# One column of SiLU at the end of places that held exponentials or roots

## Chip, cores and metric

The kernel runs on one core of one Trainium2 chip. The metric is the device time of one execution in microseconds; 2289.83 us is the median of three runs of the kernel before the change (2289.25 to 2292.66).

## What is computed

Two layers on x of shape (4, 128, 64, 64), all in float32. Layer 0 is a convolutional attention with softmax over 4096 positions. Layer 1 works on the tokens: a causal attention with SiLU on keys and values, then a mixture of experts.

```
x = x + conv_attention(group_norm(x))
t = tokens(x)                                   # (4, 4096, 128)
kv = silu(layer_norm(t) @ W_kv.T)               # 8 heads of 128, keys and values
s = sum(q * k); m = cummax(s); e = exp(s - m)
t = t + mean_over_heads(cumsum(e * v) / cumsum(e))
t = t + experts(layer_norm(t))                  # softmax gate, top 8 tokens of each of 64 experts
```

## The kernel before

The tokens of layer 1 are worked off in 32 blocks of 512 (four batches of eight). `loop` (L2254) goes over n from 6 to 37: in step n the keys of block n are made, and the values, sums and outputs of block m = n - 6. The order of TensorE, ScalarE (ACT), VectorE (DVE) and GpSimd (POOL) is the order in which the program writes the calls; SyncE's (SP's) queue of DMAs is ordered by a scheduler.

A block has named places: slots 1 to 4 and V, W, D, O, T, G between them. Two things put work into places. `later` and `point` make a list of tasks due some slots later: `scan0` to `scan4` carry a running maximum and sum over a group of four blocks, and `scan2` (L1046) holds their exponential. `make_plan` fixes the gate's work beforehand: `gate_root` (L1245, a square root, mostly in slot 4 of every fourth block), `exps` (L1400 and L1402, exponentials of the gate), `gate_norm`, `gate_turn` (transposes L1289, copy L1290), `gate_logits` and others. `last_root` (L2165) is one more root, called behind slot 4 of block 6. `run(m, place)` calls what the plan has there.

`keys` (L975, L982) multiplies a 128-token chunk by the keys' weights into the PSUM tile f_pk, and an activation with SiLU on ACT empties it into f_e1a; VectorE multiplies by the query and sums (L983, L984). `value` (L1130, L1135) does the same for values: f_pv, SiLU, f_amb. f_pk and f_pv share two PSUM buffers, taken in turn. In a step the keys of chunks 0 and 1 come first, then slot 1 (with the gate's transposes, once they are running), the values of chunks 0 and 1, and so on.

SiLU, the exponential and the square root belong to different tables of ACT. Where two instructions that follow one another need different tables, the compiler puts an ACT_TABLE_LOAD between them; the profile gives it the line of the instruction for which it loads. Copies and the activation with Identity need no load.

Of the kernel before, what the change touches and what calls it, by code (L numbers as in the profile page):

```python
# [8 lines left out]
F32 = mybir.dt.float32  # L9
AF = mybir.ActivationFunctionType  # L10
# [3 lines left out]
P = 128  # L14
# [3 lines left out]
def conv_attn_hybrid_kernel(  # L18
# [24 lines left out]
    nc = tc.nc  # L43
# [20 lines left out]
    eps5 = const.tile([P, 1], F32, tag="eps5", name="eps5")  # L64
# [763 lines left out]
    def fast():  # L828
# [14 lines left out]
        NB = len(blocks)  # L843
        env = Env()
        env.tasks, env.now = [], 0

        def later(delay, fn):
            env.tasks.append((env.now + delay, fn))

        def point():  # L850
            env.now += 1
            due = [f for at, f in env.tasks if at <= env.now]
            env.tasks = [(at, f) for at, f in env.tasks if at > env.now]
            for f in due:
                f()
# [87 lines left out]
        def scan_at(i):  # L943
            return env.e1a[:, 2 * HD + i * P : 2 * HD + (i + 1) * P]
# [8 lines left out]
        def normals(n):  # L953
            b, k = blocks[n]
            xl_of[n] = xl = env.xl_pool(f"f_xl_{n}")
            for c in range(CPB):
                i = k * CPB + c
                nc.scalar.activation(  # L958
                    xl[:, c, :], t[:, b * NCH + i, :], AF.Identity,
                    bias=ln_nb[:, b, i : i + 1], scale=ln_rs[:, b, i : i + 1],  # L960
                )
# [8 lines left out]
        def keys(n, c):  # L970
            g = n // GB
            s = scan_at(g % 2).rearrange("p (i h) -> p i h", h=NH)
            pk = ps.tile([P, 2, BLK], F32, tag="kv", name=f"f_pk_{n}_{c}", bufs=2)
            for i in range(2):
                nc.tensor.matmul(  # L975
                    pk[:, i, :], xt_at(n)[:, bass.ts(c, P)], env.wks[:, bass.ts(i, BLK)],
                    start=True, stop=True,
                )
            flat = env.e1a[:, bass.ts(env.ks_count % 2, HD)]
            env.ks_count += 1  # L980
            ks = flat.rearrange("p (h c) -> p h c", h=NH)
            nc.scalar.activation(flat, pk.rearrange("p i x -> p (i x)"), AF.Silu)  # L982
            nc.vector.tensor_mul(ks, ks, env.qb)  # L983
            nc.vector.tensor_reduce(s[:, (n % GB) * CPB + c, :], ks, AX.X, ALU.add)  # L984
            if n % GB == GB - 1 and c == CPB - 1:
                later(2, lambda: scan0(g))
# [31 lines left out]
        def row_to_column(g, by_row, what):  # L1018
            pc = sm(f"f_{what}_{g}")
            nc.tensor.matmul(pc[:, 0:1], by_row, ones[0:1, 0:1], start=True, stop=True)  # L1020
            col = fc.tile([P, 1], F32, tag=what, name=f"f_{what}c_{g}", bufs=2)
            nc.vector.tensor_copy(col, pc[:, 0:1])
            return col
# [16 lines left out]
        def scan2(g):  # L1040
            top = row_to_column(g, group[g]["m"], "mc")
            nc.vector.scalar_tensor_tensor(
                out=scan_at(DD), in0=scan_at(MM), scalar=top, in1=scan_at(SS),
                op0=ALU.max, op1=ALU.subtract,
            )
            nc.scalar.activation(scan_at(ES), scan_at(DD), AF.Exp, scale=-1.0)  # L1046
            later(1, scan2b)
            later(3, lambda: scan3(g))

# [6 lines left out]
        def scan3(g):  # L1056
            group[g]["u"] = link_rows(g, ends_to_row(g, scan_at(UL), UR, "ur"), 1, UD)
            later(1, lambda: scan4(g))
# [62 lines left out]
        def weigh_rows(m):  # L1121
            em = ready[m][0].rearrange("p z x i -> p z (x i)")
            rb = env.e2a[:, HD:].rearrange("p (z x) -> p z x", z=HH)
            nc.vector.tensor_mul(em, em, rb)
# [115 lines left out]
        def ring(m):  # L1240
            return m % NBLK

        def gate_root(m, count):
            at = slice(ring(m), ring(m) + count)
            nc.scalar.activation(  # L1245
                env.grs[:, at], env.gmv[:, at, :, 1:2].rearrange("p m c o -> p m (c o)"),
                AF.Sqrt, bias=eps5,
            )
# [62 lines left out]
        def small_tile(b, what, *shape, dtype=F32, bufs=2):  # L1311
            return env.rest.tile([P, *shape], dtype, tag=what, name=f"f_{what}_{b}", bufs=bufs)

        def flat_lg(b, k0, k1):
            return env.lg[b][:, k0:k1, :].rearrange("p k x -> p (k x)")
# [77 lines left out]
                )  # L1393

        def exps(b, j):
            st = sel[b]
            if j == 0:
                st["ce"] = ce = small_tile(b, "ce", 6)[:, 0:5]
                st["sums"] = small_tile(b, "sums", 5, bufs=1)[:, 0:4]
                nc.scalar.activation(ce, st["src"][:, 0:5], AF.Exp, bias=st["neg"])  # L1400
            lg = flat_lg(b, CPB * j, CPB * j + CPB)
            nc.scalar.activation(  # L1402
                lg, lg, AF.Exp, bias=st["neg"], accum_out=st["sums"][:, j : j + 1]
            )
# [303 lines left out]
        def slot_of(room, i):  # L1708
            return room[:, bass.ts(i, HD)]
# [452 lines left out]
                point()  # L2162

        def last_root():
            nc.scalar.activation(  # L2165
                ln_rs[:, B - 1], ln_mv[:, B - 1, :, 1:2].rearrange("p i o -> p (i o)"), AF.Sqrt,
                bias=eps5,
            )
# [14 lines left out]
        def run(i, slot):  # L2183
            for fn, args in plan.pop((i, slot), []):
                fn(*args)
# [68 lines left out]

        def loop():
            make_plan()
            normals(LAG + 1)
            for n in range(LAG, NB + LAG):
                m = n - LAG

                def slot(p):
                    if n > LAG or p > 1:
                        point()
                    run(m, p)

                if n > LAG and n < NB:
                    keys(n, 0)
                    keys(n, 1)
                slot(1)
                if m:  # L2270
                    weigh_rows(m)
                value(m, 0)
                run(m, "V")
                value(m, 1)
                slot(2)
                run(m, "W")
                if n < NB:
                    keys(n, 2)
                    keys(n, 3)
                else:  # L2280
                    value(m, 2)
                open_block(m)
                totals(0)
                if n < NB:
                    totals(1)
                    products(m, 0)
                run(m, "D")
                if 2 <= m < 6:
                    for i in range(CPB):
                        tile_stats(env.rest, B - 1, (m - 2) * NBLK + i)  # L2290
                slot(3)
                if n < NB:
                    value(m, 2)
                value(m, 3)
                if n + 1 < NB:
                    tokens(n + 1)
                if n + 2 < NB:
                    normals(n + 2)
                slot(4)
                if m == 6:  # L2300
                    last_root()
                if n >= NB:
                    totals(1)
                    products(m, 0)
                totals(2)
                run(m, "O")
                totals(3)
                close_totals(m)
                run(m, "T")
                if m + 1 < NB:  # L2310
                    weights(m + 1)
                for x4 in range(1, CPB):
                    products(m, x4)
                outputs(m)
                gate_stats(m)
                if 2 <= m < 6:
                    for i in range(CPB, 2 * CPB):
                        tile_stats(env.rest, B - 1, (m - 2) * NBLK + i)
                run(m, "G")
                if n == NB - 1:  # L2320
                    for room in (env.wks, env.held[:, bass.ts(2, HD)], slot_of(env.e1a, 0),
                                 slot_of(env.e1a, 1)):
                        load_into(room)
                if n == NB + 2:
                    load_into(slot_of(env.e1a, 2))
                    load_into(slot_of(env.ama, 2))
                if n == NB + LAG - 2:
                    for room in (slot_of(env.e1a, 3), slot_of(env.ama, 0), slot_of(env.e2a, 0)):
                        load_into(room)
            while env.tasks:  # L2330
                point()
            assert not plan, plan.keys()
# [101 lines left out]
```

## Time and profile before

| what | value |
|---|---|
| median of three runs | 2289.83 us |
| profiled execution, its own time | 2288.86 us |
| its span in the profile | 2287.0 us |
| granted TensorE clock, mean | 0.995 |
| ACT_TABLE_LOAD, one | 1283 ns |
| SiLU of keys or values, 128x1024, one | 1025 ns |
| value matmuls L1130, busy and idle before | 239.4 and 6.2 us |

The span is the stretch that the profile's instructions fill; 1.9 us of the execution lie around it. A row of the profile gives line, engine, operation and tiles, then the number of instructions, busy time and the mean of one in ns, and after the second bar the idle time of the engine before them and what ended it. Layer 0 fills the span up to about 1515 us, the attention loop goes on to about 2180 us, the experts to about 2257 us, and the stores of the output end it.

### The profile page before, as it was taken

The page shows a single profiled execution, that of the slowest core. Times are in us where ns is not written, and L with a number is a line of the kernel's source. Part 1 is how long each engine was busy: PE and PEld are TensorE (multiplying, and loading weights), DVE is VectorE, ACT ScalarE, POOL GpSimd, SP SyncE. Part 2 cuts the span into 40 slices and gives each one's busy share as a digit, 9 for nine tenths or more (in the row PEclk, how much of TensorE's full clock was granted, in tenths as well). Part 3 has the DMA queues.
Part 4 walks back from the last instruction along what each step waited for, and adds up shares of the span by engine and source line. Part 5 has one row for each costly group of instructions (what it writes and reads, how often), then busy time and mean ns, then how long its engine had stood idle before and what let it go on. Part 6 is the DMA issues. An engine that isn't in the chain of part 4 may idle for free. (4 is left out here: it accounts for less than half of the span.)

```text
span 2287.0 us, 42915 instructions
## 1 busy us (share of the span) xinstructions
PE 2223.4 (97%) x18224; PEld 1147.4 (50%) x18224; DVE 1460.2 (64%) x2380; ACT 1091.6 (48%) x1328; POOL 175.9 (8%) x380
## 2 busy tenths in 40 slices
PE   7999999999999999999999999999999999999997
PEld 3644444444444444444444444456556555666663
DVE  7666665655666556556555666667877777776643
ACT  3344334443433443334444554445565676565651
POOL 0000000000000000000000000012121121223311
PEclk9999999999999999999999999999999999999999
DMA  2100010000010000001000000020211211313589
GB/s 68 42 12 12 14 46 9 17 9 9 9 53 9 9 9 17 9 9 44 9 5 5 5 5 10 6 49 27 65 45 40 67 50 41 95 55 110 169 298 343
DMA packets 79418, 108.95 MB, mean 48 GB/s; under 512 B 9072, under 2 KB 44912, under 8 KB 78960
## 3 DMA queue, kind: packets, MB, share of 16 engines
q1 hardware_dynamic: 78128, 104.01, 14.6%
q8 instruction: 145, 2.38, 0.4%
q0 software_dynamic: 512, 1.05, 0.2%
q10 hardware_dynamic: 576, 1.05, 0.1%
q14 instruction: 57, 0.47, 0.1%
HBM read 80.64 MB, written 19.14 MB: 44 GB/s over the span
## 5 line engine op out<-in xcount | busy, mean ns | idle before, releaser
L2033 PE MATMUL av<-pr,am 64*128 64x512 f32 x4096 | 980.0, 593 | 8.1 <-ACT pr L2013 8.1
L2013 ACT ACTIVATE pr<-sc 128x1024 f32<-128x1024 f32 x512 | 523.9, 1025 | 779.4 <-PE sc L2008 763.4
L2020 DVE TENSOR_TENSOR acc<-acc,pr 128x1024 f32<-128x1024 f32 x480 | 587.4, 1224 | 472.3 <-ACT pr L2013 468.7
L2033 PEld LDWEIGHTS av<-pr,am 64*128 64x128 f32 x4096 | 402.1, 187 | 480.3 <-issue 455.7
L2008 PE MATMUL sc<-e,e 64*128 64x512 f32 x2048 | 536.7, 593 | 3.9 <-DMA e<-side 3.9
L2008 PEld LDWEIGHTS sc<-e,e 64*128 64x128 f32 x2048 | 202.7, 188 | 236.5 <-issue 230.9
L1130 PE MATMUL f_pv<-f_held,f_ama 128*32 128x256 f32 x4096 | 239.4, 383 | 6.2 <-ACT f_e1a L982 5.1
L975 PE MATMUL f_pk<-f_held,f_ama 128*128 128x512 f32 x512 | 234.5, 602 | 0.0
L1135 ACT ACTIVATE f_amb<-f_pv 128x1024 f32<-128x1024 f32 x128 | 131.1, 1025 | 133.3 <-PE f_pv L1130 131.3
L983 DVE TENSOR_TENSOR f_e1a<-f_e1a,f_held 128x1024 f32<-128x1024 f32 x128 | 156.5, 1223 | 44.1 <-ACT f_e1a L982 43.8
L982 ACT ACTIVATE f_e1a<-f_pk 128x1024 f32<-128x1024 f32 x128 | 129.8, 1025 | 108.5 <-PE f_pk L975 54.4
L1130 PEld LDWEIGHTS f_pv<-f_held,f_ama 128*32 128x32 f32 x4096 | 129.9, 110 | 101.8 <-issue 12.0
L984 DVE TENSOR_REDUCE f_e1a<-f_e1a 128x8 f32<-128x1024 f32 x128 | 155.3, 1218 | 3.5
L975 PEld LDWEIGHTS f_pk<-f_held,f_ama 128*128 128x128 f32 x512 | 92.5, 190 | 108.3 <-issue 100.9
L1094 POOL COPY f_held<-f_e1a 32x32 f32<-32x32 f32 x128 | 30.7, 240 | 900.3 <-DVE f_e1a L1076 553.5
L1153 PE MATMUL f_pt<-f_amb,f_held 128*32 128x128 f32 x1920 | 84.1, 277 | 0.8 <-ACT f_amb L1135 0.8
L920 POOL MEMSET f_held<- 128x1024 f32 x1 | 1.0, 957 | 1033.6 <-DVE xn L1946 1033.6
L1153 PEld LDWEIGHTS f_pt<-f_amb,f_held 128*32 128x32 f32 x1920 | 60.4, 109 | 10.5 <-issue 5.2
L1194 DVE TENSOR_TENSOR t<-t,f_po 128x512 f32<-128x512 f32 (+1 forms) x33 | 22.1, 671 | 56.4 <-PE f_po L1188 56.4
L958 ACT ACTIVATE f_xl<-t,ln_nb,ln_rs 128x128 f32<-128x128 f32 x128 | 52.9, 491 | 0.8 <-PE pa L1981 0.8
L1277 ACT ACTIVATE f_x<-t,f_gnb,f_grs 128x128 f32<-128x128 f32 x122 | 49.7, 483 | 0.4 <-DVE f_grs L1255 0.4
L2017 DVE COPY acc<-pr 128x1024 f32<-128x1024 f32 x32 | 22.2, 694 | 39.3 <-ACT pr L2013 39.3
(304 smaller groups left out, 1777.4 us busy)
## 6 DMA issues: line engine op xcount, KB each, us to landing
f_e2a<-f_rd SPq DMA_DIRECT2D x128, 128.0 KB, 3.1
xr<-in_xtok_dram SPq DMA_DIRECT2D x32, 256.0 KB, 2.8
f_table<-f_x SPq DMA_DIRECT2D x62, 128.0 KB, 2.5
out_dram<-t SPq DMA_DIRECT2D x14, 512.0 KB, 3.8
x<-in_x_dram SPq DMA_DIRECT2D x12, 512.0 KB, 4.8
e<-e SPq DMA_DIRECT2D x32, 128.0 KB, 2.2
f_ama<-f_rd SPq DMA_DIRECT2D x16, 256.0 KB, 3.9
f_e1b<-f_rd SPq DMA_DIRECT2D x16, 256.0 KB, 4.1
```

The source lines that it names most:

```text
L958: nc.scalar.activation(xl[:, c, :], t[:, b * NCH + i, :], AF.Identity, bias=ln_nb[:, b, i : i + 1], scale=ln_rs[:, b, i : i + 1],)
L975: nc.tensor.matmul(pk[:, i, :], xt_at(n)[:, bass.ts(c, P)], env.wks[:, bass.ts(i, BLK)], start=True, stop=True,)
L982: nc.scalar.activation(flat, pk.rearrange("p i x -> p (i x)"), AF.Silu)
L983: nc.vector.tensor_mul(ks, ks, env.qb)
L984: nc.vector.tensor_reduce(s[:, (n % GB) * CPB + c, :], ks, AX.X, ALU.add)
L1130: nc.tensor.matmul(pv[a * CH : (a + 1) * CH, i, :], xt_at(m)[:, bass.ts(c * NA + i, CH)], env.wvs[:, bass.ts(a, HH * C)], start=True, stop ...
L1135: nc.scalar.activation(env.amb[:, bass.ts(c, HD)], pv.rearrange("p i x -> p (i x)"), AF.Silu)
L1153: nc.tensor.matmul(env.pt[i * CH : (i + 1) * CH, :], lhs, rhs, start=i not in env.begun, stop=False, skip_group_check=True,)
L2008: nc.tensor.matmul(sc[:, u, :], e2[halves[u], p, :], e1[halves[u], cols], start=True, stop=True,)
L2013: nc.scalar.activation(pr, sc, AF.Exp)
L2020: nc.vector.tensor_add(acc, acc, pr)
L2033: nc.tensor.matmul(av, am[h, j, :], pr[h, u, :], start=(j == 0), stop=(j == NCH - 1))
```

## The change

A one-column scratch tile and a flag are added. Every function that uses an exponential or a root on ACT sets the flag. At the end of slots 1 to 4 and of the places D and G, if the flag is set, ACT gets an activation with SiLU on one column (`eps5`, written to the scratch tile) and the flag is cleared; the last block is left out. `last_root` is called inside slot 4, before the new instruction.

```
+        def silu_table():
+            if env.other:
+                nc.scalar.activation(env.spare, eps5, AF.Silu)
+            env.other = False
+
         def gate_root(m, count):
+            env.other = True
...
         def loop():
             make_plan()
+            env.spare = env.rest.tile([P, 1], F32, tag="spare", name="f_spare")
+            env.other = False
...
                     run(m, p)
+                    if p == 4 and m == 6:
+                        last_root()
+                    if m + 1 < NB:
+                        silu_table()
...
                 run(m, "D")
+                if m + 1 < NB:
+                    silu_table()
...
                 slot(4)
-                if m == 6:
-                    last_root()
...
                 run(m, "G")
+                if m + 1 < NB:
+                    silu_table()
```

`env.other = True` is also added to `scan2` (behind its exponential), `exps` and `last_root`. 18 instructions are added in all.

More of the change, by code (lines that the diff above doesn't have):

```diff
@@ L1241, in ring @@
             return m % NBLK
+        def silu_table():
+            if env.other:
+                nc.scalar.activation(env.spare, eps5, AF.Silu)
+            env.other = False
         def gate_root(m, count):
+            env.other = True
             at = slice(ring(m), ring(m) + count)
@@ L1395, in exps @@
         def exps(b, j):
+            env.other = True
             st = sel[b]
@@ L2164, in last_root @@
         def last_root():
+            env.other = True
             nc.scalar.activation(
```

## The prediction

> **What bounds the kernel now.** I began with the page's engine table and the granted clock.
>
> ```profile
> PE 2223.4 (97%) x18224; PEld 1147.4 (50%) x18224; DVE 1460.2 (64%) x2380; ACT 1091.6 (48%) x1328; POOL 175.9 (8%) x380
> ```
>
> TensorE sets the time: 97% busy, its clock row at 9 in every slice. ScalarE (ACT) is about half idle, so what ACT does counts only where TensorE waits for it. The list of TensorE's waits says where that is:
>
> ```profile
> PE f_pv L1130 <- ACT f_e1a L982: 5.1, 14, 0.7
> ...
> PE f_pv L1130 <- ACT f_amb L1135: 0.9, 2, 0.8
> ...
> PE f_pt L1153 <- ACT f_amb L1135: 0.8, 2, 0.5
> ```
>
> Columns: microseconds in total, times, the longest. Value matmuls (L1130) wait 14 times for the keys' SiLU (L982), because keys and values share two PSUM buffers: the first value tile needs the buffer that the first key SiLU empties. To see what these 14 have in common I listed ACT's groups by line:
>
> ```profile
> L982 ACT ACT_TABLE_LOAD x21 | 26.9, 1283 | 17.3 <-issue 11.5 <-PE f_pk L975 5.7
> ...
> L1135 ACT ACT_TABLE_LOAD x5 | 6.4, 1283 | 3.3 <-PE f_pv L1130 3.2
> ...
> L1251 ACT ACTIVATE f_gnb<-eps 128x1 f32<-128x1 f32 x1 | 0.2, 203 | 0.0
> ```
>
> A table load takes 1283 ns. The last numbers of its row matter more: ACT is idle 17.3 us before the 21 loads of L982. The loads themselves wait for TensorE. One block of the loop, ACT in order of time, then TensorE over the same stretch:
>
> ```profile
> 1747.39 1.28 ACT L1046 ACT_TABLE_LOAD   x1
> 1748.68 0.31 ACT L1046 ACTIVATE f_e1a<-f_e1a 128x128 f32<-128x128 f32 x1
> 1750.34 1.28 ACT L982 ACT_TABLE_LOAD   x1 [1.35 <-PE f_pk L975]
> 1751.63 1.94 ACT L982 ACTIVATE f_e1a<-f_pk 128x1024 f32<-128x1024 f32 x2
> ```
>
> ```profile
> 1748.27 3.70 PE L975 MATMUL f_pk<-f_held,f_ama 128*128 128x512 f32 x8
> 1751.81 0.60 PE L1289 MATMUL f_gtr<-ident,f_x 128*128 128x128 f32 x4
> 1752.71 0.64 PE L1130 MATMUL f_pv<-f_held,f_ama 128*32 128x256 f32 x8 [0.30 <-ACT f_e1a L982]
> ```
>
> The exponential ends at 1748.99, ACT idles 1.35 us until the keys' product is there, and only then loads SiLU's table: SiLU starts 1.30 us late, its first tile is out at 1752.65, and TensorE goes on at 1752.71. A block without a load, for comparison:
>
> ```profile
> 1683.70 3.70 PE L975 MATMUL f_pk<-f_held,f_ama 128*128 128x512 f32 x8
> 1687.24 0.60 PE L1289 MATMUL f_gtr<-ident,f_x 128*128 128x128 f32 x4
> 1687.77 3.66 PE L1130 MATMUL f_pv<-f_held,f_ama 128*32 128x256 f32 x64
> ```
>
> From the first keys matmul to the first value matmul it takes 4.07 us here and 4.44 there: a block with a load loses 0.37 us (the 0.30 us gap plus the 0.07 us by which matmuls otherwise overlap).
>
> **The change, part by part.** The lists of instructions of both built programs show 18 added activations of one column on ACT and not one more table load (105 in each). Each of the 18 loads now stands before the small instruction, with no wait on it, where before it carried the wait for the product. TensorE, VectorE and POOL keep their order. Moving the root of the last batch into the place leaves ACT's order as it was.
>
> *The small instruction* has a row of the same form, L1251: 203 ns. Bounds: 0.1 us (neighbouring activations overlap by some 0.1 us in the timeline) to 0.3 us (the 128x5 exponential, 299 ns). After the end of the exponential or root ACT needs 0.02 + 1.28 + 0.20 minus some overlap, about 1.45 us, until it is ready for the next SiLU. Where it idled 1.2 us or more before the load this costs nothing; the cover is that idle time, and without it each place costs 0.1 to 0.3 us.
>
> *Fourteen places before key SiLUs*, from the timeline around each load (first keys to first value matmul):
> - Two early blocks (values at 1579.90, 1622.53), where no gate transposes stand between: 4.44 and 4.43 us against 3.63 without a load. ACT idled 1.38 and 1.24 us, so SiLU can start 1.1 to 1.2 us sooner, more than the 0.80 needed: 2 x 0.80 = 1.6 us.
> - Ten blocks like the one shown, 4.42 to 4.44 against 4.07, idle 1.03 to 2.76 us: 10 x 0.36 = 3.6 us.
> - One (1926.48) with an exponential of 1024 columns in the same place: idle only 0.23 us, so 0.23 - 0.15 = 0.08 us.
> - One (1663.39) with three loads in a row and no idle time: the small instruction comes on top, -0.14 us (-0.3 to 0).
>
> *Four late places* before value SiLUs: at 2096.43 the load goes into the 1.08 us in which ACT waited for a transpose, and the value wait of 0.756 us goes (+0.82 with the overlap); at 2119.34 nobody waits, 0; at 2149.11 ACT had 0.17 us to spare and the load now stands before a copy, -0.15; at 2157.08 ACT idled 0.85 us and a wait of 0.451 us at L1153 goes, +0.5.
>
> Sum: 1.6 + 3.6 + 0.08 - 0.14 + 0.82 - 0.15 + 0.5 = 6.3 us.
>
> *SP's queue* has one group of reorderings: in five blocks a store of the gate's table changes place with the third of four loads of f_e2a. The last of the four stays last, and in those blocks the VectorE product that reads them (L1124) starts 13.7 to 18 us after the last issue: 0.
>
> *The end.* Is the gain kept? I take all of it; the bounds are 0 and 6.3. The windows near the end:
>
> ```profile
> 2100.00:2190.00 90.00, 83.28 (x1574) 57.42 (x1566) 52.93 (x171) 58.28 (x88) 26.04 (x42) 0.96 0.56 177
> 2190.00:2200.00 10.00, 8.49 (x58) 4.60 (x58) 3.79 (x13) 5.91 (x12) 0.00 (x0) 0.83 0.42 126
> 2200.00:2250.00 50.00, 46.34 (x682) 30.08 (x682) 13.75 (x42) 21.28 (x48) 4.32 (x25) 1.00 1.04 372
> ```
>
> The last two columns are the DMA engines' share and GB/s. From 2200 the experts' weights fill the DMA engines (1.04), but this stretch starts with the first reload, issued at 2196.20 when the first expert matmuls (2194.26) free their room; before it the share is 0.56 and 0.42. So it starts earlier when TensorE comes earlier. The largest stall on the way, 2.56 us at 2133.08 for VectorE, hangs on a VectorE run that began at 2125.84 on TensorE's L1188, and shifts too.
>
> The profiled execution took 2288.86 us (span 2287.0 and 1.9 around it); less 6.3 that is 2282.6. The median is 0.97 above it, so 2289.83 - 6.3 = 2283.5.
>
> The Trainium skill (ScalarE: Activation LUTs, What ACT_TABLE_LOAD costs) gives a switch 1283 ns for the load and some 1380 ns of drain, 2.66 us together; here the load agrees and the drain isn't seen: the next activation starts 0.01 us after the load's end (1663.39 to 1664.68). By its figure each of the ten blocks would lose 1.38 us more than the 0.37 they do lose, and the estimate would be 14 us more gain, which the 4.44 us excludes.
>
> **Rivals.**
>
> *The end takes it back* (chance 0.15). TensorE waits 2.3 us for weights of the experts between 2238 and 2250; if preloads issued at 2175 to 2192 don't come earlier, the gain turns into such waits. All of it: 2289.8; half: 2286.7. Against it: those preloads wait in SP's queue for TensorE and ACT.
>
> *Nothing is gained* (0.05). The number of loads stays, ACT's busy time grows by 18 x 0.2 = 3.7 us; if the value matmuls were held by something else that comes at the same time, 2289.8. Against it: SiLU's first tile ends 0.06 us before every one of the waits. The Trainium skill (ScalarE: Activation LUTs, Table sets: the hidden batching unit) advises batching functions by set, which this change doesn't do; by that rule alone nothing is won.
>
> *Slower: the load doesn't go ahead* (0.10). If the small instruction is held as the SiLU was, behind ACT's own earlier instructions or a wait, the load stays where it is and 0.2 us comes on top at 17 places where TensorE waits or nearly does: 3.4 us, 2293.2, and with 0.3 us 2294.9. It decides where ACT's end of exponential plus 1.45 us passes the product's arrival by over 1 us. For it: the one place with three loads. Against it: loads without a wait start 0.02 us after the instruction before (1747.39).
>
> **How the numbers follow.** Forecast 0.70, the rivals 0.15, 0.05 and 0.10. The forecast's own range is 2282.0 to 2285.5. A measurement of this kernel can tell about 0.2% (4.6 us): faster is under 2285.25. Faster: 0.64 of the forecast and 0.02 of the first rival, 0.66. Slower: 0.07 of the last rival. The rest, 0.27, is the same. The range goes from 2281.5 (some 2 us more, if weight loads that wait on the same SiLU hide more) to 2290.5, which leaves the slower rival out.
>
> **What would show it.** Right: the wait of L1130 for L982 falls from 5.1 us to under 0.5 us, first keys to first value matmul is 4.07 us in the load blocks, the loads stand next to the exponential's end without idle time before them, and the first reload is issued some 6 us sooner. Wrong: the loads still start with the product's arrival, or the first reload comes sooner but waits for DMA grow at the experts (L1754, L1784).

## The result, and the profile after

| | before | after |
|---|---|---|
| median of 7 runs each | 2289.25 us (2285.61 to 2292.66) | 2280.07 us (2277.33 to 2283.81) |
| profiled execution, span | 2288.86, 2287.0 us | 2283.81, 2281.9 us |
| granted clock of that execution | 0.995 | 0.994 |

The ratio is 0.9962 with an interval of 0.9949 to 0.9974: 6.0 to 11.7 us less. A second series, in the experiments below, gave 0.9972 (0.9962 to 0.9983), 3.9 to 8.7 us. Both hold together between 6.0 and 8.7. The forecast said 6.3 us and 2283.5 us, with 2281.5 as the low end of its range; the first median lies 1.4 us below that end, the second (2281.68) just inside it. So the direction was right, and the size has to be explained.

The list of TensorE's waits of the changed kernel (microseconds in total, times, the longest):

```profile
PE f_pw L1334 <- DVE f_both L1347: 2.5, 1, 2.5
...
PE f_pl L1303 <- ACT f_spare L1246: 1.1, 1, 1.1
...
PE f_pv L1131 <- ACT f_e1a L982: 0.8, 2, 0.7
```

The 14 waits of 5.1 us for the keys' SiLU have become two of 0.8 us (the place with three loads has 0.7 of it). The 2.5 us for f_both have stayed. The 1.1 us in the middle are put down to the new instruction because its semaphore is the last one that the profile has; but what these matmuls follow in each of the two profiles is VectorE's L1307, by 0.14 to 0.15 us (its end at 2113.56 and their start at 2113.71 here), and in the second profile they start at 2112.67, ahead of the new instruction at 2113.31. The VectorE product before L1307 waited 5.7 us here for a DMA of f_e2a; in the second profile it waits 4.8 us, as in before, and TensorE 0.2: a late transfer of one execution.

ACT's groups of the changed kernel by line (count, busy us, mean ns of one; then the idle time before them):

```profile
L1246 ACT ACT_TABLE_LOAD x18 | 23.1, 1283 | 0.1
...
L982 ACT ACT_TABLE_LOAD x7 | 9.0, 1283 | 0.1
...
L1246 ACT ACTIVATE f_spare<-eps 128x1 f32<-128x1 f32 x18 | 3.7, 203 | 0.2
```

Of the 21 loads that stood at L982 after 17.3 us of idle time, 14 now stand at the new instruction, with 0.1 us of idle time before all 18 there. The new instruction takes 203 ns. The profile has 70 table loads in either kernel, so none was added; the 105 of the prediction was counted in the built programs, and no view of the profile shows that number.

The same block as in the prediction, ACT and then TensorE, in the changed kernel (start, duration, engine, line; in brackets the idle time before and what ended it):

```profile
1746.78 1.28 ACT L1046 ACT_TABLE_LOAD   x1
1748.08 0.31 ACT L1046 ACTIVATE f_e1a<-f_e1a 128x128 f32<-128x128 f32 x1
1748.39 1.28 ACT L1246 ACT_TABLE_LOAD   x1
1749.69 0.20 ACT L1246 ACTIVATE f_spare<-eps 128x1 f32<-128x1 f32 x1
1749.80 1.00 ACT L982 ACTIVATE f_e1a<-f_pk 128x1024 f32<-128x1024 f32 x1
```

```profile
1747.69 3.70 PE L975 MATMUL f_pk<-f_held,f_ama 128*128 128x512 f32 x8
1751.22 0.60 PE L1296 MATMUL f_gtr<-ident,f_x 128*128 128x128 f32 x4
1751.75 1.50 PE L1131 MATMUL f_pv<-f_held,f_ama 128*32 128x256 f32 x24
```

The load starts 0.01 us after the exponential's end, not 1.35 us later with the product. The first SiLU ends 3.11 us after the first keys matmul (1750.80 and 1747.69) and not 4.38 as before, so TensorE goes from the transposes straight to the values: from the first keys matmul to the first value matmul it is 4.06 us, where it was 4.44. In the two early blocks it is 3.63. One of the ten common blocks (values at 1972.74 in before) comes down only to 4.19 us, because two more matmuls of the gate (L1471) stand there between the transposes and the values.

**One ruler for all profiles.** The work up to the loop's second step takes 1533 to 1541 us in different executions, so spans hide a gain of some microseconds. The table below counts from the first value matmul of that step (1538.11 in the profile of before) to the same instruction of TensorE's order in each profile, found by aligning the orders. The mark at 2062.00 is the first value matmul of the last block that has keys; the text calls it the last keys. In microseconds:

```
mark (before's time)    before  before, again  after  after, again
1840.30                 302.19  302.18         299.21 299.21
2062.00, last keys      523.90  523.38         517.12 517.12
2100.57                 562.47  561.66         554.61 554.28
2160.02                 621.91  621.77         613.66 611.82
end of the program      748.89  748.11         742.55 740.71
```

Up to 1840 two profiles of one kernel agree to 0.01 us. The two columns of before differ at 2062 by 0.5 us through one gap of TensorE that only the first of them has. By this ruler the change gains 6.3 us until the last keys (523.4 less 517.1) and about 6.9 us until the end (748.5 less 741.6, each a mean of two; 6.3 to 8.2 by the pair taken).

**Why the clock has to be looked at.** The trace's record of the granted clock shows stretches at half rate, 3.41, 6.83 or 10.24 us long. In before two lie between 2100 and 2200 us, at 2132.7 (6.8 us) and 2194.1 (3.4); in after at 2127.7 (3.4) and 2185.7 (6.8). At 0.50 of the clock each costs half its length while TensorE has work. They differ from execution to execution, in layer 0 too, and with them the time: of 26 runs of before, those at a mean clock of 0.994 took 2290.6 us in the mean, at 0.995 2289.2, at 0.997 2285.7, and the one at 0.998 2282.2. At equal clock the changed kernel is some 7.5 to 8.5 us faster (0.995: 2280.7, the mean of four runs in both series, against 2289.2; 0.997: 2278.2, of two runs, against 2285.7).

### The profile page after: what moved, and what is told of

It is laid out like the page before. It is cut to its first block, busy times and chain, and to the rows that moved or that the text cites. A ratio compares the mean times of both kernels' runs of the same rounds, so it can differ in the third digit from the quotient of the medians.

```text
span 2281.9 us, 42933 instructions
## 1 busy us (share of the span) xinstructions
PE 2223.0 (97%) x18224; PEld 1147.8 (50%) x18224; DVE 1460.6 (64%) x2380; ACT 1093.8 (48%) x1346; POOL 173.8 (8%) x380
## 5 line engine op out<-in xcount | busy, mean ns | idle before, releaser
L982 ACT ACTIVATE f_e1a<-f_pk 128x1024 f32<-128x1024 f32 x128 | 130.6, 1023 | 116.1 <-PE f_pk L975 57.3
```

## The experiments

Two theories were to be told apart. A: the gain is 7 to 9 us, more than the sum of the prediction, because a SiLU that is late also makes VectorE late, and that holds TensorE again further on. B: the sum of 6.3 us was right, and what is above it is the scatter of the runs. The expectations name further rivals by letters, each with what it would give.

### Both kernels again

No edit.

> The changed kernel once more, for the spread. Theory A (loads moved ahead of the product, plus a follow-on gain through VectorE's queue; the scatter between runs comes from stretches in which TensorE's clock is halved): the value matmuls wait under 1 us in total for the keys' SiLU, first keys to first value matmul is 4.07 us in the blocks with a load, and the gain over the kernel before is 7 to 9 us in the mean of the runs, with the faster runs showing the higher granted clock. Rival B (the 6.3 us of the prediction were right and the first runs lucky): 5.5 to 6.5 us.

> The kernel before once more, as a second profile and for the noise of a comparison. Both theories: 14 waits of 5.1 us in total of L1130 for L982 as in the first profile, ratio 1.000 within 0.001. Theory A: outside the attention loop the two profiles of this kernel differ by 1 to 3 us, where halved-clock stretches fall differently; inside the loop, up to 2100 us, by under 0.3 us. Rival B' (waits of the loop come and go by chance): the waits of L1066 for L1300 at 1855 and 2032 are gone or elsewhere.

Measured: the changed kernel 2281.68 us (8 runs, 2279.66 to 2282.58), the kernel before 2288.9 (26 runs); ratio 0.9972 (0.9962 to 0.9983), 3.9 to 8.7 us. The kernel before against itself: 1.0008 (0.9998 to 1.0019). The waits and the 4.07 us came out alike in each second profile, and so did two waits of 0.35 us of TensorE for VectorE at f_etr that only before has: they are no chance of one profile. That the loop of before would repeat to 0.3 us up to 2100 did not come true: it was 0.5 to 0.8 us, 0.5 by the gap named above and 0.3 in the value matmuls between 2080 and 2088, of which more below. The times alone exclude neither A nor B; the ruler favours A.

### Is it SiLU's table? The small instruction with another function

```
-                nc.scalar.activation(env.spare, eps5, AF.Silu)
+                nc.scalar.activation(env.spare, eps5, AF.Identity)
```

> The 18 small instructions use Identity, which needs no table load. Theory A: SiLU's loads stand behind the product's arrival again, L1131 waits about 5 us for L982 in 14 places, and the time is that of the kernel before: 0 to 1 us of difference. Rival C (the gain comes from something else that the edit brings, the order of SP's queue or the place of tiles): most of the 8.7 us stays, ratio near 0.996.

Measured: 2287.55 us (10 runs), ratio 0.9995 (0.9986 to 1.0004): no gain. ACT's groups by line of this kernel, and then TensorE's waits:

```profile
L982 ACT ACT_TABLE_LOAD x21 | 26.9, 1283 | 15.6 <-issue 10.2 <-PE f_pk L975 5.1
...
L1246 ACT ACTIVATE f_spare<-eps 128x1 f32<-128x1 f32 x18 | 3.4, 187 | 0.0
```

```profile
PE f_pv L1131 <- ACT f_e1a L982: 5.2, 14, 0.7
...
PE f_etr L1067 <- DVE f_lg L1307: 0.7, 2, 0.3
```

With a function that needs no table the 18 instructions stand in the same places, but the 21 loads are back at L982 behind idle time, and the 14 waits are back to 0.1 us. So the gain comes from the place of the load and from nothing else in the edit (the moved root is in this kernel as well). The instructions themselves cost nothing that the loop shows.

### Does VectorE carry part of it? No early load at two of the ten blocks

```
                     if p == 4 and m == 6:
                         last_root()
+                    if p == 4 and m in (14, 22):
+                        env.other = False
                     if m + 1 < NB:
                         silu_table()
```

> The change without its small instruction at slot 4 of blocks 14 and 22, the last blocks before the gate's exponentials. Theory A (a late SiLU makes VectorE late, which runs without a pause from the keys to the gate's logits, so that TensorE waits once more 15 us later): in each of these two places first keys to first value matmul goes back to 4.43 us and the wait of 0.35 us for the gate's logits at the transposes of the exponentials comes back, so 1.5 to 2.0 us of the lead are lost in the profile. Rival B' (those later waits come by chance): 0.7 us lost, 2 x 0.36, and no wait at the transposes.

Measured: at the last keys 518.69 us against 517.12, so two places lost 1.57 us, and not the 2 x 0.37 = 0.74 us that the value matmuls wait there. The difference, 0.83 us, is at TensorE's f_etr, whose two waits of 0.35 us are there again. (Its one time of 2277.97 us says nothing against that: its layer 0 was shorter and its clock 0.997.) How a late SiLU gets there is seen in VectorE's order of time. First before, then after:

```profile
1840.28 1.23 DVE L983 TENSOR_TENSOR f_e1a<-f_e1a,f_held 128x1024 f32<-128x1024 f32 x1 [1.86 <-ACT f_e1a L982]
...
1854.60 0.47 DVE L1300 TENSOR_SCALAR f_lg<-f_pl,f_gbs 128x256 f32<-128x256 f32 x1
...
1855.92 0.16 DVE L1072 COPY f_ucc<-f_etr 128x1 f32<-128x1 f32 x1 [0.39 <-PE f_etr L1070]
```

```profile
1837.69 1.23 DVE L983 TENSOR_TENSOR f_e1a<-f_e1a,f_held 128x1024 f32<-128x1024 f32 x1 [0.59 <-ACT f_e1a L982]
...
1852.02 0.47 DVE L1307 TENSOR_SCALAR f_lg<-f_pl,f_gbs 128x256 f32<-128x256 f32 x1
...
1853.82 0.16 DVE L1073 COPY f_ucc<-f_etr 128x1 f32<-128x1 f32 x1 [0.87 <-PE f_etr L1071]
```

VectorE idles 1.86 us for the first SiLU before, 0.59 us after. From there it runs with no pause above 0.04 us to the gate's logits (14.32 and 14.33 us from the first product to L1300 or L1307): the whole delay is still in its queue at the end. Before, TensorE reaches f_etr first and stands 0.35 us:

```profile
1855.12 0.46 PE L1066 MATMUL f_etr<-ident,f_e1a 128*32 128x32 f32 x32 [0.35 <-DVE f_lg L1300]
```

After, it is VectorE that waits for TensorE (0.87 us at L1073). This is theory A's mechanism, and it happens in two blocks: 2 x 0.41 us.

The profiles show a third place of the kind, which this kernel leaves as it is in after. VectorE and then TensorE in before, in the block of 1972.74:

```profile
1972.72 1.23 DVE L983 TENSOR_TENSOR f_e1a<-f_e1a,f_held 128x1024 f32<-128x1024 f32 x1 [1.85 <-ACT f_e1a L982]
...
1989.11 0.27 DVE L1170 COPY f_e1b<-f_pt 128x128 f32<-128x128 f32 x1
```

```profile
1989.47 1.08 PE L1188 MATMUL f_po<-f_e1b 128*32 128x128 f32 x32
```

VectorE idles 1.85 us for the first SiLU (0.70 in after), then works 16.65 us with no pause above 0.04 us, and TensorE's L1188 starts just behind the copy that it reads. In after the copy is done at 1984.79 and the same matmuls start at 1985.35, behind no wait. From the value matmuls at 1982.63 to the next keys TensorE takes 8.78 to 8.79 us in the four profiles in which this block's SiLU is late (both of before, and of the kernels with Identity and with the merge alone below) and 8.49 to 8.50 us in the eight others: 0.30 us. No kernel takes away this one load alone.

### Which places count? Only those of the keys

```
-                    if m + 1 < NB:
+                    if n + 1 < NB:
                         silu_table()
...
                 run(m, "D")
-                if m + 1 < NB:
-                    silu_table()
...
                 run(m, "G")
-                if m + 1 < NB:
-                    silu_table()
```

> The change without its four late small instructions, those ahead of value SiLUs. Theory A: up to the last keys (before: 2062) the lead over the kernel before is that of the whole change, 6.3 to 6.8 us, and the late places give 0.9 us by 2100 and 1 to 2 us by 2160, which are missing here. Rival D (the late places give nothing that lasts, because the gate's loads and VectorE set the pace there): the lead at 2160 is that of the whole change, 8 us, within 0.5 us.

Measured: 517.12 us at the last keys, as in after; 555.60 at 2100, where after has 554.28 and 554.61; 615.98 at 2160, where after has 611.82 and 613.66. The one time, 2286.88 us at a clock of 0.992, has a half-rate stretch more than after in this part. So the late places are worth something, but this pair doesn't say how much: the stretches cover it. A cleaner pair follows below.

### Place or wait? The small instruction behind the product

```
+            if getattr(env, "owed", False):
+                env.owed = False
+                nc.scalar.activation(env.spare, pk[:, 0, 0:1], AF.Silu)
...
-                nc.scalar.activation(env.spare, eps5, AF.Silu)
+                env.owed = True
```

(The same three lines stand before the values' SiLU, with `pv`.) The small instruction now reads the first column of the product itself, so it can't run before the product is there.

> The small instruction stands just ahead of the SiLU and reads one column of its product, so it waits for the product; the built program leaves the table load ahead of it without a wait. Theory A (the load's place alone counts): first keys to first value matmul is 4.07 us in the ten common blocks as with the change, since 0.1 to 0.2 us more on ACT lie within the 1 us that SiLU has to spare there, and the lead at the last keys is 6.0 to 6.8 us. Rival E (the load waits with it on the chip): 4.5 to 4.65 us in these blocks and no lead, the loop 2 to 3 us slower than before.

Measured: no loss. 517.11 us at the last keys, and 4.07 us in the blocks, except the one that has 4.19 in after too. ACT's order of time in this kernel says why:

```profile
1742.42 0.31 ACT L1049 ACTIVATE f_e1a<-f_e1a 128x128 f32<-128x128 f32 x1
1742.75 1.28 ACT L984 ACT_TABLE_LOAD   x1
1744.04 0.17 ACT L984 ACTIVATE f_spare<-f_pk 128x1 f32<-128x1 f32 x1
1744.11 1.02 ACT L985 ACTIVATE f_e1a<-f_pk 128x1024 f32<-128x1024 f32 x1
```

The load still starts without idle time behind the exponential, 1.3 us before the small instruction reads the product; in the last block with keys ACT even idles 1.4 us between its load and the small instruction, which waits there for the product. In the built program the load carries no wait when the instruction that it precedes is the small one, even if that one waits. So what the small instruction reads doesn't matter; that it keeps the wait off the load does. Why the compiler hangs the wait of the large SiLU on its load and that of the small one not, these runs don't show.

### What is left: the stall for f_both, one slot later

After the change the longest wait of the loop is TensorE's 2.5 us for f_both. The merge of the gate's halves, which makes f_both needed, is put one slot later.

```
-            at(NB - 3, 2, merge_halves, last)
+            at(NB - 3, 3, merge_halves, last)
```

> The change, and the merge of the gate's two halves of the third batch moved from slot 2 to slot 3 of block 29, so that TensorE doesn't wait 2.5 us there for VectorE's search. Theory A (after a stall of this length TensorE's clock is halved for 3.4 or 6.8 us, which costs half of that): the stall is under 0.5 us, no halved stretch begins near 2128, and the time from the first value matmul to 2160 falls by 2.5 + 1.7 = 4.2 us against the change alone, 2.5 to 5.9 by the length of the stretch; the whole 3 to 5 us faster than the change. Rival F (VectorE sets the pace there): the stall moves to the gate's exponentials or the next block and 0 to 1 us is gained.

Measured: 2275.22 us (4 runs, 2273.29 to 2279.03) against 2287.66 for the kernel before on the same chip; ratio 0.9950 (0.9935 to 0.9965), 8 to 15 us. TensorE at the merge, in after and then in this kernel:

```profile
2128.06 0.62 PE L1334 MATMUL f_pw<-f_both,ident 128*64 128x16 f32 x8 [2.54 <-DVE f_both L1347]
2128.61 3.14 PE L1131 MATMUL f_pv<-f_held,f_ama 128*32 128x256 f32 x32
```

```profile
2123.17 0.41 PE L1334 MATMUL f_pw<-f_both,ident 128*64 128x16 f32 x8 [0.62 <-DVE f_lg L1307]
2123.51 1.93 PE L1131 MATMUL f_pv<-f_held,f_ama 128*32 128x256 f32 x32
```

The stall falls from 2.54 to 0.62 us (under 0.5 was expected), and the same 32 value matmuls behind it take 1.93 us, not 3.14. The windows behind the stall show what that is: in after, and then in this kernel (stretch, us, then busy us of TensorE, its weight loads, VectorE, ACT and GpSimd, then the granted clock, the DMA share and GB/s):

```profile
2128.00:2131.00 3.00, 2.94 (x32) 1.70 (x36) 2.75 (x12) 0.00 (x0) 0.00 (x0) 0.50 0.36 140
```

```profile
2126.00:2129.00 3.00, 2.94 (x97) 2.66 (x99) 1.26 (x5) 2.97 (x4) 1.25 (x2) 1.00 0.62 139
```

Behind the stall the clock is 0.50 in after and 1.00 here. At 2160 this kernel has 608.38 us where the two profiles of after have 611.82 and 613.66: 3.4 to 5.3 us (4.2 were expected, 2.5 to 5.9), of which 1.9 are the stall itself and some 1.7 the half-rate stretch of 3.4 us. Beside the change's two ratios, 0.9962 and 0.9972, the 0.9950 is 2.7 to 5.0 us more (3 to 5 were expected).

### The same, and the root away from the block with three loads

```
-            at(7, 1, last_close)
+            at(9, 1, last_close)
...
-                    if p == 4 and m == 6:
+                    if p == 4 and m == 8:
                         last_root()
```

(with the merge one slot later as above). The one place where the change couldn't help has three loads in a row; the root that makes one of them is called two blocks later.

> As the run before, and the root of the last batch moved from block 6 to the end of slot 4 of block 8, where the gate's root has loaded the same table, with its closing in block 9: one load less, and no place with three loads in a row. Theory A: the block at 1665 goes from 4.79 to 4.07 us, so 0.7 us more than the run before in the profile, too little to be seen in the times; against the kernel before 10 to 12 us in all. Rival F as above: 7 to 8 us in all.

Measured: the place, at 1665, has 4.07 us and one load less (69 in the profile), and at 1840 the loop is 0.75 us ahead of the last kernel (298.48 against 299.23). Its time, 2277.19 us (5 runs), ratio 0.9959 (0.9945 to 0.9973), can't be told from that of the last kernel: 6.2 to 12.6 us gained against 8 to 15. 10 to 12 us were expected and 9.4 are the middle.

### The late places, without the stall

The edits of "only those of the keys" and of "one slot later" together.

> The merge moved to slot 3, as two runs before, and the small instructions without the four late places: the worth of these four without the stall near 2130 and the halved clock behind it. The run with the merge moved and all 18 reached the mark of before's 2160 at 608.4 us after the first value matmul of the loop. Theory A (the late places save what the prediction worked out, 0.8 and 0.5 less 0.15): 609.4 to 609.8. Theory G (they save more, since VectorE and the gate's chain follow ACT here too): 610.4 or later. Rival D (nothing that lasts): 608.4 to 608.9.

Measured: 610.19 us at 2160 against 608.38 with all 18 instructions, and neither kernel has a half-rate stretch before that mark: 1.81 us, between the two expectations. On the ruler, the 1.81 us come in three parts.

- 0.43 us lie in the value matmuls from 2080.03 to 2087.57, which take 7.45 us here and 7.02 with all 18. TensorE does them before the first of the four late instructions runs, and they differ as much in profiles of one kernel: 7.54 and 7.25 us in before, 7.41 and 7.08 in after, 7.02 to 7.99 over all twelve profiles. So this part isn't the four instructions'.
- 0.96 us lie between 2087.57 and 2100.57, where before had its load at 2096: 13.00 or 13.01 us in the six profiles without an early load there, 12.04 or 12.05 in the six with it.
- 0.40 us come from the three other places.

Without the first part the mark would be at 609.76, in theory A's range.

### The merge alone, without the change

```
-            at(NB - 3, 2, merge_halves, last)
+            at(NB - 3, 3, merge_halves, last)
```

(in the kernel before)

> The kernel before with the merge moved to slot 3 and no small instruction. Theory A (the two edits act on different waits): 3 to 6 us faster than before, the mark of 2160 at 615.5 to 618.5 us after the first value matmul (before: 621.8 to 621.9), and 14 waits of L1130 for L982 as before. Rival H (the gain of the merge hangs on the earlier table loads): under 1.5 us.

Measured: 2284.27 us (10 runs) against 2288.8 (13 runs), ratio 0.9977 (0.9965 to 0.9988), 2.7 to 8 us. The 14 waits of 5.1 us are all there, the stall is 0.61 us, and there is no half-rate stretch behind it. Within the noise the two edits add up: 4.5 us here (2288.8 less 2284.3) and some 7.5 by the change make 12.0, beside the 12.4 us that both gained together (2287.66 less 2275.22).

This kernel and that of "one slot later" differ by the change alone, and neither has a half-rate stretch before 2160: the cleanest pair for the change. On the ruler they stand 6.2 us apart at the last keys (523.39 and 517.15), 8.3 at 2160 (616.68 and 608.38), 8.0 at the first expert matmuls, near 2194 (650.91 and 642.92), and 7.3 at the end (744.01 and 736.68). But 0.88 of the 8.3 are the value matmuls from 2080.03 to 2087.57 once more (7.90 and 7.02 us), which differ without the change too. So up to 2160 the change is worth 7.4 us in this pair.

## Where the prediction held, and the step that failed

**The bound and the mechanism: right.** TensorE's waits for the keys' SiLU were real and came from the load's place. Of the 17.3 us of idle time before the 21 loads the row puts only 5.7 to TensorE's product and 11.5 to issue; that all of it came from the loads' wait is shown by the 0.1 us that were left. The kernel with Identity brings all 14 waits back with the same instructions in the same places, and the one with the small instruction behind the product shows that only the load's place counts.

**The small instruction: right.** 203 ns, as the row of the same form said; in the place with three loads it costs 0.08 us, where 0.14 was put down, and in the place with the long exponential 0.13 us are gained where 0.08 was.

**Two early blocks and ten others: right as far as the value matmuls go, but for one of the ten.** 3.63 us in the two, so 1.6 us. Nine of the ten come to 4.07; the tenth comes to 4.19, because the prediction compared it with a block that lacks its two matmuls of L1463. So the ten give 3.45 us and not 3.6.

**The end: right.** In the clean pair the first reload of the experts' weights is issued 8.0 us sooner on the ruler, 8.0 of the 8.3 us are there at the first expert matmuls, and 7.3 at the program's end; the experts' waits for DMA at L1784 are 2.3 us in before and 2.2 in after. From a mark near 2198 to the end two profiles of one kernel differ by about 1 us (748.89 - 660.08 = 88.8 and 748.11 - 658.36 = 89.8 for before), so the last 0.7 us can't be told from none. The rival by which the end takes it back falls, and so do the two others: something is gained, and the load does go ahead, in each of the places.

**SP's queue: no cost seen.** VectorE waits for f_e2a in the loop 7.9 and 9.0 us in the two profiles of before, 6.9 and 8.3 in the two of after, most of it at one place near 2110 in each.

**The step that failed is the path behind the value matmuls, which the sum put at nothing.** The prediction ended each place at the value matmuls that wait for SiLU. It looked at TensorE and ACT and not at VectorE, which reads every one of those tiles too. There the delay goes on through 14 to 17 us of work without a pause and comes out where TensorE waits for VectorE: 0.82 us at f_etr in two blocks, shown by the kernel that takes the early load away there, and 0.30 us at L1188 in a third, read from the profiles. With it the fourteen places give 1.60 + 3.45 + 0.13 - 0.08 + 0.82 + 0.30 = 6.2 us and not 5.1, and the ruler has 6.2 in the clean pair.

**The four late places: nearly right.** 0.96 us where 0.82 was put down, and 0.2 to 0.4 us for the three others (0.35 was). Together that makes 7.4 to 7.6 us where the sum said 6.3. It agrees with the 7.4 of the clean pair up to 2160 and with the 7.2 us between the medians of the second series (2288.9 and 2281.68).

**The low end of the range** added 2 us for unknown overlaps of weight loads, and nothing for the scatter of the median. The runs of the changed kernel lie between 2277.3 and 2283.8 us, because one half-rate stretch more or less is 1.7 us or more; the medians of two series are 2280.07 and 2281.68. Of the 3.4 us between the forecast and the first median, 0.6 are the median of before, which came down from 2289.83 to 2289.25 with four more runs, 1.2 are the sum (7.5 us instead of 6.3), and the remaining 1.6 are put down to this scatter: 2289.25 - 7.5 = 2281.75, where the second median is. That the first series fell on the low side is taken for chance; no run shows a cause.

**What stays open.** What holds the value matmuls between 2080 and 2088 longer in some executions: no row names it. The third place of VectorE's delay has no kernel of its own. The half-rate stretches don't account for every mark: the two profiles of before stand alike at 2160 (621.91 and 621.77) with a stretch of 6.8 us in the one and 3.4 us in the other; part of it is that in the second VectorE waits 6.0 us and not 4.8 for f_e2a near 2110. Why layer 0 has more of these stretches in one execution than in the next wasn't tried.

## What to carry to other kernels

A table load can carry the semaphore wait of the activation that it serves; where an idle time stands before such loads, one column of the needed function in that idle time moves the load there. Price a late engine at every engine that reads its result, and follow a queue without pauses to its end: the delay comes out at the first instruction that another engine waits for. A stall of 2.5 us of TensorE can cost twice its length by the clock behind it, so it is worth moving its cause first, and differences of a few microseconds are read at equal clock or from a mark inside the program.

## What the runs showed of the hardware that was not expected

The clock of TensorE was halved in the middle of a stall of 2.5 us, some 2.1 us after the stall had begun (stall from 2130.5, half rate from 2132.7 in before), and it came back after 3.41 or 6.83 us, though TensorE had work again from 2133.08. The windows of before:

```profile
2133.00:2136.00 3.00, 2.92 (x32) 1.70 (x36) 2.77 (x12) 0.00 (x0) 0.00 (x0) 0.50 0.38 147
2136.00:2139.00 3.00, 3.00 (x34) 2.02 (x26) 0.52 (x4) 1.60 (x3) 1.01 (x1) 0.50 0.24 72
```

TensorE is busy for 5.92 of these 6 us, at half rate throughout. A stall of 0.6 us in the same place left the clock at 1.00. The Trainium skill (TensorE: Matmul & The Clock Gate, Part 1: The HAM clock gate) has the clock go to half after an idle window of about 3.4 us that runs freely. The lengths here (3.41, 6.83, 10.24 us) agree with such a window and the 0.50 with its half rate; that the stall need be as long as the window doesn't agree, since 2.5 us were enough.

A load's length, 1283 ns, was the same in all profiles, and the next activation began 0.01 us behind it (1749.67 to 1749.69 here).
